# Two graph layers with attention and experts on one core: the bf16 copy of the adjacency made by casting transfers, attention products in quarters of the array, and an order of work read from a list

## The chip, the cores and the metric

The kernel runs on one core of a Trainium2 chip (trn2) as one program. The metric is the device time of that core in microseconds. The kernel before took 1467.53 us, the median of 3 runs (1466.63 to 1470.84).

The engines are named as in the profile: PE is TensorE (matmuls), PEld its weight loads, DVE is VectorE, ACT is ScalarE, POOL is GpSimd, SP is SyncE, which here issues DMAs only.

## The reference

There are N = 2708 nodes with 256 features and a matrix `adj` of 2708 x 2708 in float32, about 1.2% of it not zero, with values up to 1e9. Two layers follow one another; each is a graph part and an expert part.

```python
# layer 0
x = x + gnn0(layernorm(x), adj)          # softmax(leaky_relu(f1 + f2.T) + adj) @ h + bias
x = x + ffn0(layernorm(x))               # causal attention (4 heads, 2 key heads, 64 wide) over
                                         # 2708 tokens, then 8 experts, the best 2 for each token
# layer 1
x = x + gnn1(layernorm(x), adj)          # graph attention: mask = (adj != 0) | eye
x = x + ffn1(layernorm(x))               # 8 experts, the best 2 for each token
```

Since layer 0 adds `adj`, with its huge values, to the logits, the softmax of a row is one at the row's largest entry. The kernel finds that entry's index and gathers one row of `h`. (A general path for other data stands at the end of the program and is not taken.) Layer 1 needs only where `adj` isn't zero.

## The kernel before

The nodes lie in 22 tiles of 128 rows (the last has 20). There are four stages in order: `first` (layer 0's graph part, attention and routing), the experts of layer 0, `second` (layer 1's graph part and routing), the experts of layer 1.

**`first`**, for each pair of tiles in `project` and for each tile in `tile_in`:

1. `project`: statistics of x on DVE (`stats`), a power on POOL, transposes on PE (`turn`), `h` = x times the centred weights on PE (`times`, L949), scaled on ACT (`out_`) and stored to the DRAM tensor `hd`. The centred weights come from one PE product with `allones` (`centre`, L893 and L897).
2. `load` (SP, L990): one tile of 128 rows of `adj`, 10,832 bytes each, into one of three parts of `arena`.
3. `top` (DVE MAX8, L995) and `index` (DVE FIND_INDEX8, L999): the largest entry of each row and its place.
4. `narrow` (ACT, L1009) copies the tile to bf16 in two halves, with memsets of the padding on POOL (L1006, L1008), and `save` (SP, L1012) stores each half to the DRAM tensor `mb`. `narrow` needs the last store of `hd` to be issued. A part of `arena` is free for the next load when both `index` and `narrow` are done (the buffer names `adj0..2` and `low0..2`).
5. `fetch` (POOL, L1017): an indirect gather from `hd` that adds to x. It needs all of `hd`.
6. Statistics, norm, transposes, and the product with the query, key and value weights (PE, L1047); the rotation on POOL (L804 to L806, L1064); transposes into `qT` and `kT` (PE, L1070).

**Attention**, `pair(t0)`, for two tiles of queries t0, t0+1 against the tiles of keys up to t0+1, taken two at a time. For each tile of keys, `scores` multiplies 64 rows of `kT` and `qT` for each of the 2 key heads (PE, L1121: 64 rows, 128 columns, 512 wide, into the bank pair `st`), `exps` is on ACT (L1127), `mask` on POOL for the last two. `values` multiplies 128 rows of `V` and `e` into the bank `o` (PE, L1147: 128 rows, 64 columns for each key head). For the first three pairs (`PE_SUMS`) the softmax's sums are made by PE too (L1154, into bank `zs`); for the others DVE adds the tiles `e` up (`sums`, L1161 and L1166) and one PE product spreads the sums (L1199). Then `leave` copies `o` on ACT (L1188), DVE takes the reciprocal (L1204), POOL multiplies (`weigh`, L1208), PE projects (L1222), DVE and POOL add to x, and SP stores it. A product in float32 appears as two matmul instructions.

`route` runs after pairs 4, 10, 16, 18 and 20 (t0): logits (L424), the choice of two experts on DVE, and `send`, two indirect scatters for each tile on POOL (L1830) into the experts' lists `xs`. A few blocks of expert work (`early_blocks`) start within the stage. `nobody` (L1288) are PE fillers without use, put into gaps that the plan foresees; they multiply `allones` by `before`, a triangular matrix that DVE finishes (L232).

**The order of the work** around the change is set by `Plan`. Each step is added with an engine, an assumed length, what it needs, the buffers that it takes and gives, and a rank; `issue` then walks a model clock, and of the steps that can start soonest issues the one with the smallest rank. The instructions stand in the program in that order, each engine works its own in order, and semaphores keep the dependences:

```python
            soon = min(at for at, _ in can)
            first = min((s for at, s in can if at <= soon), key=lambda s: s["rank"])
```

**`second`** reads `mb` with transposing DMAs into bf16 masks, and aggregates over 22 tiles for groups of six (PE, L1603). It is ordered by a `Plan` of its own.

Of the kernel before, what the change touches and what calls it, by code (L numbers as in the profile page):

```python
# [20 lines left out]
P = 128  # L21
N = 2708
# [51 lines left out]

class Plan:
# [8 lines left out]
    UNIT = 0.24  # L84
    FILL = 0.75
    GAP_MIN = 1.0
# [38 lines left out]
    def issue(self, behind=0.0):  # L125
# [25 lines left out]
def adj_ffn_kernel(ctx, tc, x, adj, vecs, bias_rows, tab, w_gnn0, w_gnn1, wqkv, wo,  # L151
# [41 lines left out]

    ident = const.tile([P, P], F32, name="ident")
# [33 lines left out]
    allones = const.tile([P, P], F32, name="allones")  # L228
    nc.gpsimd.memset(allones, 1.0)

# [138 lines left out]

    def route(add, tiles, ready, copied, cleared, layer, XB, xs, pool, turn_tile, turn_bank, gate_tile, gate_bank, rank):  # L370
# [127 lines left out]
        if layer == 0:  # L498
            a = [add("ACT", 0.6, lambda t=t: squares(t), [ready[t - t0]], rank=rank) for t in tiles]
            a = add("DVE", 0.3, mean, a, rank=rank)  # L500
            scaled = add("POOL", 0.9, power, [a], rank=rank)
        last = None
        for pair in pairs:
# [10 lines left out]
            if gate_tile is None:  # L514
                a = add("ACT", 0.25, lambda pair=pair: keep(pair), [a], give=[turn_bank], rank=rank)
            last = a
        a = add("DVE", 3.2, choose, [last], rank=rank)
        b = add("ACT", 0.5, exps, [a], rank=rank)
# [3 lines left out]
        return [add("POOL", 2.7, lambda t=t: send(t), [b, c] + cleared, rank=rank + 6, lands=2.0) for t in tiles]  # L522


    def some_blocks(add, layer, blocks, fetched, needs, weights, xs, acc, new, named, rank):

        joins = []
        for k, (e, j, before) in enumerate(blocks):
# [68 lines left out]
            a = add("ACT", 0.7, back, [a], take=[names["xT"]], give=[names["mm"]], rank=r)  # L597
# [3 lines left out]
            a = add("ACT", 1.4, gate, [a], take=[names["sl"], names["hT"]], rank=r)  # L601
            a = add("DVE", 1.4, times, [a], give=names["up"] + [names["sl"]], rank=r)
# [4 lines left out]
            joins.append(add("POOL", 1.6, join, [a], give=[names["ys"]], rank=r))  # L607
        return joins

    def early_blocks(add, layer, needs, sent, *rest):  # L610
        blocks = [(e, j, (needs if layer == 0 else []) + sum([sent[t] for t in sent if t < before_t], []))
                  for e, j, before_t in EARLY[layer]]
# [196 lines left out]
    def first(X, XB, norms, tops, hd, mb, xs, acc, arena, load_weights):  # L809
# [11 lines left out]
        with ExitStack() as s:  # L821
# [24 lines left out]
            def tr_tile():  # L846
                return mm_tile().rearrange("p (k c) -> p k c", c=P)

            plan = Plan(mm=2, mv=4, ix=4, tb=6, st=2, o=1, zs=1, e=4, xg=3, hT=3,
                        z=2, qk=2, es=1, ob=2, yT=2, mb=2, rT=1, adj0=1, adj1=1, adj2=1, low0=1, low1=1, low2=1)  # L850
# [396 lines left out]
            for t in range(NT):  # L1247
                tile_in(t)
# [1194 lines left out]
```

## Time and profile before

| | us |
|---|---|
| Median of 3 runs | 1467.53 |
| The profiled execution, its own time | 1465.13 |
| Its span (first to last instruction) | 1463.3 |
| PE busy | 1385.9 (95%) |
| DVE busy | 775.9 (53%) |
| ACT busy | 555.3 (38%) |
| POOL busy | 525.3 (36%) |
| Granted TensorE clock, mean | 0.984 |

The busy shares are means over four stages with different limits; a stage is to be read from its own window. A busy PE is not PE at its peak: matmuls are pipelined, and a change of their shape costs time that the busy share doesn't show. The stages end at about 509.5, 804, 1148 and 1463.3 us.

### The profile page before, as it was taken

Reading aid. Unit: us, or ns where it says so; the run is one execution under the profiler, and the core shown is the slowest. Engines: PE = TensorE matmul, PEld = TensorE weight load, DVE = VectorE, ACT = ScalarE, POOL = GpSimd, SP = SyncE. Lnnn points to the kernel's source line nnn. Section 1 sums busy time; section 2 is a strip of 40 time slices with the busy share of each in tenths; the row PEclk is TensorE's granted clock in tenths of the full one; section 3 lists DMA queues with packets and bytes.
Section 4 is the critical chain, followed back from the end, with each engine's and each line's share of the span. In section 5 each row is a group of like instructions: output and inputs, shape, how many; then the busy total and the mean of one; then the engine's idle time right before and its main releaser. Section 6 shows DMA issues by size and latency. Waiting matters only on the chain.

```text
span 1463.3 us, 20902 instructions
## 1 busy us (share of the span) xinstructions
PE 1385.9 (95%) x7218; PEld 1006.3 (69%) x7218; DVE 775.9 (53%) x1680; ACT 555.3 (38%) x1104; POOL 525.3 (36%) x677
## 2 busy tenths in 40 slices
PE   6988989989999999999999899999999999999996
PEld 5643433433343888888788878888768888878885
DVE  5688999985676432222222474768565322322221
ACT  2576867655545322222221444434432211111110
POOL 5576668874224312222222210022334222222222
PEclk9899999999999999999999999999999999999998
DMA  7588756540001277777512770616321687666211
GB/s 268 192 290 287 252 197 226 158 155 31 8 16 64 46 205 185 168 175 197 105 18 26 159 166 1 133 39 151 108 73 58 148 214 187 194 185 129 24 19 21
DMA packets 260056, 193.05 MB, mean 132 GB/s; under 512 B 168008, under 2 KB 232104, under 8 KB 257232
## 3 DMA queue, kind: packets, MB, share of 16 engines
q1 hardware_dynamic: 235638, 162.32, 38.0%
q0 software_dynamic: 20032, 25.71, 9.7%
q10 hardware_dynamic: 4270, 3.58, 0.8%
q8 instruction: 59, 0.97, 0.3%
q14 instruction: 57, 0.47, 0.1%
HBM read 119.81 MB, written 56.11 MB: 120 GB/s over the span
## 4 chain that ended last, share of the span: by engine, by line
PE 77%; DVE 8%; POOL 6%; DMA 5%; issue 2%; ACT 1%; SPq 0%; POOLq 0%; DVEq 0%; ACTq 0%
PE pup L2115 23%; PE po L1603 15%; PE y L2130 13%; PE o L1147 4%; PE stt L1121 4%; PE up L562 3%; DMA X<-hd,ix 3%; PE pup L2146 3%; PE y L2180 1%; DVE yT L1204 1%; DVE es L1166 1%; PE po L949 1%; DVE ix L999 1%; POOL ra L804 1%; DVE tops L995 1%
## 5 line engine op out<-in xcount | busy, mean ns | idle before, releaser
L2115 PE MATMUL pup<-xTs,arena 128*128 128x256 f32 (+2 forms) x1320 | 249.7, 348 | 0.6 <-ACT xTs L2098 0.6
L2115 PEld LDWEIGHTS pup<-xTs,arena 128*128 128x128 f32 (+1 forms) x1320 | 218.5, 189 | 27.2 <-PE y L2180 1.5
L1603 PE MATMUL po<-hb,PT 128*128 128x257 f32 (+2 forms) x968 | 227.6, 389 | 2.9 <-DVE PT L1596 2.9
L2119 ACT ACTIVATE sl<-pup 128x256 f32<-128x256 f32 (+1 forms) x210 | 73.5, 350 | 368.9 <-PE pup L2115 325.4
L1603 PEld LDWEIGHTS po<-hb,PT 128*128 128x128 f32 (+2 forms) x968 | 176.7, 189 | 42.8 <-issue 13.3
L2120 DVE TENSOR_TENSOR hT<-sl,pup 128x256 f32<-128x256 f32 (+1 forms) x210 | 79.6, 380 | 225.8 <-ACT sl L2119 220.5
L1127 ACT ACTIVATE e<-stt 128x1024 f32<-128x1024 f32 (+1 forms) x132 | 125.5, 986 | 93.5 <-PE stt L1121 63.8
L1166 DVE TENSOR_TENSOR es<-es,e 128x1024 f32<-128x1024 f32 x104 | 137.8, 1325 | 29.8 <-ACT e L1127 22.0
L622 POOL DMA_INDIRECT out<-ys,XR x44 | 68.0, 1545 | 234.2 <-DVE ys L2133 149.5
L622 POOL DMA_INDIRECT acc<-ys,XR x44 | 68.3, 1553 | 215.4 <-DVE ys L2133 120.8
L1121 PE MATMUL stt<-qT,kT 64*128 64x512 f32 (+1 forms) x528 | 133.4, 616 | 4.3 <-ACT e L1127 3.9
L2130 PE MATMUL y<-arena,hT 128*128 128x256 f32 x612 | 137.3, 380 | 0.0
L2130 PEld LDWEIGHTS y<-arena,hT 128*128 128x128 f32 x612 | 114.6, 190 | 19.7 <-DVE hid L2154 4.9
L1830 POOL DMA_INDIRECT xs<-XR,place x88 | 93.2, 1059 | 91.8 <-DVE mk L1590 40.2
L1147 PE MATMUL o<-e,V 128*64 128x512 f32 (+1 forms) x528 | 122.4, 586 | 0.0
L1581 ACT ACTIVATE E<-sb,dcol 128x768 f32<-128x768 f32 (+1 forms) x88 | 75.3, 859 | 108.4 <-DVE PT L1596 106.5
L2133 DVE TENSOR_SCALAR ys<-y,XR 128x256 f32<-128x256 f32 x71 | 34.4, 484 | 133.7 <-PE y L2130 133.7
L2115 PE MATMUL pup<-xTs,room 128*128 128x256 f32 (+3 forms) x528 | 99.9, 346 | 0.0
L1121 PEld LDWEIGHTS stt<-qT,kT 64*128 64x128 f32 x528 | 44.7, 188 | 76.5 <-issue 63.0
L2115 PEld LDWEIGHTS pup<-xTs,room 128*128 128x128 f32 (+1 forms) x528 | 85.4, 189 | 9.8 <-PE y L2180 0.8
L1147 PEld LDWEIGHTS o<-e,V 128*64 128x64 f32 x528 | 32.9, 136 | 68.5 <-issue 53.2
L995 DVE MAX8 tops<-arena 128x8 f32<-128x2708 f32 (+1 forms) x22 | 65.3, 2970 | 1.5 <-DMA arena<-in_adj 1.5
(319 smaller groups left out, 1972.1 us busy)
## 6 DMA issues: line engine op xcount, KB each, us to landing
more<-in_w SPq DMA_DIRECT2D x48, 640.0 KB
arena<-in_adj SPq DMA_DIRECT2D x21, 1354.0 KB
arena<-in_w SPq DMA_DIRECT2D x36, 640.0 KB
mb<-mb SPq DMA_DIRECT2D x44, 352.0 KB
xs<-none SPq DMA_DIRECT2D x16, 536.0 KB
room<-in_w SPq DMA_DIRECT2D x12, 640.0 KB
pieces<-xs SPq DMA_DIRECT2D x200, 32.0 KB
acc<-X SPq DMA_DIRECT2D x21, 128.0 KB
```

Source lines behind the costliest of these rows:

```text
L622: i = nc.gpsimd.indirect_dma_start(out=acc[:, :], out_offset=bass.IndirectOffsetOnAxis(ap=tokens.bitcast(I32), axis=0), in_=ys, in_offset= ...
L995: nc.vector.max(out=tops[:r, t, :], in_=v["a"][:r])
L1121: nc.tensor.matmul(st[:r, g, c0(sb):], kT[a:b, sb * P:sb * P + r], qT[a:b, t0 + (sb == t0 + 1):t0 + 2, :, :], start=True, stop=True)
L1127: nc.scalar.activation(e[:r, :, c0(sb):], v[sb, "st"][:r, :, c0(sb):], AF.Exp, scale=1.0 / HD ** 0.5)
L1147: nc.tensor.matmul(v["o"][g * HD:(g + 1) * HD, c:], V[:r, sb, g * HD:(g + 1) * HD], v[sb][:r, g, c:], start=(n + i == 0), stop=(n + i == t ...
L1166: nc.vector.tensor_tensor(es, es, v[sb][:r, :, c:], ALU.add)
L1581: nc.scalar.activation(e[:q, :n], sb[:q, i0:i1], AF.Exp, bias=dcol[:q, j:j + 1], scale=SLOPE - 1.0)
L1603: nc.tensor.matmul(v["po", i][:r, :F], v["PT", j][:q, a:a + r], hb[:q, j, :], start=(j == 0), stop=(j == NT - 1))
L1830: i = nc.gpsimd.indirect_dma_start(out=xs[:, :], out_offset=bass.IndirectOffsetOnAxis(ap=at, axis=0), in_=src, in_offset=None)
L2115: nc.tensor.matmul(pp[:to, i, :B, :], wn[:, c, :], xT[:, c, :B, :], start=(c == 0), stop=(c == KC - 1))
L2120: nc.vector.tensor_tensor(hT[:, n, :B, :], sl[:, :B, :], pp[:, 1, :B, :], ALU.mult)
L2130: nc.tensor.matmul(y, hT[:, n, b, :], w[3][:, n, :], start=(n == 0), stop=(n == NHC - 1))
```

## The change

**Casting transfers, late.** `narrow` and `save` are gone. `cast` issues on POOL one DMA for each tile from `adj` in DRAM to `mb` in DRAM, float32 to bf16. All 22 need the last `load` in the plan, and each the one before it. `blank` stores the padding of `mb` once, on SP. The index goes into one tile `ixs` for all 22. An `arena` part is free after `index`.

**Quarters.** For all but the first three pairs, `scores` splits the keys of a tile in two halves of 64 columns, and `values` its rows in two halves of 64, so that both have the shape 64 rows by 64 columns. The second halves of `values` go to a second bank, `zs`, so that a pair takes `o` and `zs`. `leave` for these pairs is two DVE instructions, a copy of one bank and an addition of the other. `route` no longer uses `zs` for its logits but the turning bank and a copy (`keep`).

**Order.** Both plans take ranks from a list, `ORDERS[0]` for `first` and `ORDERS[1]` for `second`. Many assumed lengths differ, and some steps have added needs (the earlier choice of experts; the stores of x for the early blocks). Two steps without an instruction stand at each plan's end.

**Start.** x is loaded in five pieces, statistics and powers of `project` go by pairs of tiles, `tab` has a load of its own, and fillers multiply `allones` by itself; `allones` is set near the start of POOL's work. Fillers are counted with 0.22 for 0.24, 0.85 for 0.75 and gaps from 0.7 for 1.0.

```diff
+ORDERS = [[int(n) for n in text.split()] for text in (
...
-    UNIT = 0.24
-    FILL = 0.75
-    GAP_MIN = 1.0
+    UNIT = 0.22
+    FILL = 0.85
+    GAP_MIN = 0.7
...
+    def issue(self, order, behind=0.0):
+        for step, n in zip(self.steps, order):
+            step["rank"] = n
...
+            loads, ends = [], (2, 6, 14, NT - 1)
+            for a, b in zip((0,) + ends, ends):
...
-                def narrow(h):
-                    v["m", h] = m = adjp.tile([P, HALF], BF16, tag="mb", name="mb", bufs=2)
...
-                    nc.scalar.copy(m[:r, :b - a], v["a"][:r, a:b])
-                def save(h):
-                    nc.sync.dma_start(out=mb[t * P:(t + 1) * P, h * HALF:(h + 1) * HALF], in_=v["m", h])
+                def cast():
+                    nc.gpsimd.dma_start(out=mb[t * P:t * P + r, :N], in_=adj[t * P:t * P + r, :])
...
-                a = loaded[t] = add("SP", 5.8, load, take=[f"adj{t % 3}", f"low{t % 3}", "tb"], rank=rank,
-                                    lands=1.5)
+                a = loaded[t] = add("SP", 3.6, load, take=[f"adj{t % 3}"], rank=rank - 2.0, lands=2.0)
+                tb = add("SP", 0.4, load_tb, take=["tb"], rank=rank, lands=2.2)
...
+                def keys(sb):
+                    r = rows(sb)
+                    return [(0, r)] if on_pe else [(p, min(p + HD, r)) for p in range(0, r, HD)]
...
-                            nc.tensor.matmul(st[:r, g, c0(sb):], kT[a:b, sb * P:sb * P + r],
-                                             qT[a:b, t0 + (sb == t0 + 1):t0 + 2, :, :], start=True, stop=True)
+                            for p, q in keys(sb):
+                                nc.tensor.matmul(st[p:q, g, c0(sb):], kT[a:b, sb * P + p:sb * P + q],
+                                                 qT[a:b, t0 + (sb == t0 + 1):t0 + 2, :, :], start=True, stop=True)
...
-                                nc.tensor.matmul(v["o"][g * HD:(g + 1) * HD, c:], V[:r, sb, g * HD:(g + 1) * HD],
-                                                 v[sb][:r, g, c:], start=(n + i == 0), stop=(n + i == t0 + 1))
+                                for p, q in keys(sb):
+                                    to = v["o2" if p else "o"]
+                                    nc.tensor.matmul(to[g * HD:(g + 1) * HD, c:], V[p:q, sb, g * HD:(g + 1) * HD],
+                                                     v[sb][p:q, g, c:], start=(n + i == 0), stop=(n + i == t0 + 1))
...
-                    nc.scalar.copy(v["ob"], v["o"])
-                    if on_pe:
+                    if not on_pe:
+                        nc.vector.tensor_copy(v["ob"], v["o"])
+                        nc.vector.tensor_tensor(v["ob"], v["ob"], v["o2"], ALU.add)
+                    else:
+                        nc.scalar.copy(v["ob"], v["o"])
...
+            for t, cast in enumerate(casts):
+                last = add("POOL", 1.2, cast, [loaded[NT - 1], last], rank=NT + 0.5 * t, lands=6.0)
...
-                        nc.tensor.matmul(nobody[:, :P], allones, before, start=True, stop=True)
+                        nc.tensor.matmul(nobody[:, :P], allones, allones, start=True, stop=True)
...
-                plan.issue()
+                plan.issue(ORDERS[0])
```

## The prediction

> **What bounds the kernel now.** I read the page's busy shares first, then the windows by stage, the groups of the first stage, the waits of VectorE, and single matmuls. Four stages follow one another: the first (layer 0 up to its experts, 0 to 509.5 us), the experts of layer 0 (to 804), the second (layer 1 up to its experts, to 1148) and the experts of layer 1. The experts are untouched by the diff and TensorE is busy throughout them.
>
> The windows below cut the first stage at the ends of the 1st, 7th and 11th attention reciprocal (L1204, one for each pair of query tiles), and add the second stage. Columns: window, its length, then busy us (instructions) of PE, PEld, DVE, ACT and POOL, granted clock, DMA share, GB/s.
> ```profile
> 0.00:97.65 97.65, 74.96 (x374) 55.61 (x374) 65.82 (x132) 49.35 (x97) 61.30 (x115) 0.91 0.72 242
> 97.65:297.50 199.85, 179.74 (x798) 74.81 (x798) 189.86 (x185) 145.03 (x252) 150.57 (x192) 0.97 0.70 229
> 297.50:480.00 182.50, 174.29 (x796) 68.12 (x795) 124.38 (x170) 92.62 (x145) 77.18 (x105) 1.00 0.15 50
> 480.00:509.50 29.50, 27.05 (x192) 24.26 (x191) 10.79 (x45) 9.71 (x23) 12.79 (x17) 1.00 0.24 50
> 804.00:1148.00 344.00, 334.16 (x1773) 280.15 (x1774) 209.42 (x645) 136.93 (x251) 88.56 (x150) 0.99 0.41 99
> ```
> From 97.65 to 297.5 us VectorE is busy 95% of the time: it sets the pace there, TensorE is close behind. From 297.5 to 480 TensorE is (8.2 us idle; VectorE is busy 68%). In that second part the DMA engines lie nearly idle (share 0.15), in the first they carry 0.70.
>
> The groups show what fills the two engines:
> ```profile
> L1121 PE MATMUL stt<-qT,kT 64*128 64x512 f32 (+1 forms) x528 | 133.4, 616 | 4.3 <-ACT e L1127 3.9 <-issue 0.3
> L1147 PE MATMUL o<-e,V 128*64 128x512 f32 (+1 forms) x528 | 122.4, 586 | 0.0
> ```
> ```profile
> L1166 DVE TENSOR_TENSOR es<-es,e 128x1024 f32<-128x1024 f32 x104 | 137.8, 1325 | 29.8 <-ACT e L1127 22.0 <-issue 1.0 <-DVE es L1166 0.5
> L999 DVE FIND_INDEX8 ix<-tops,arena 128x8 uint32<-128x2708 f32 (+1 forms) x22 | 65.4, 2972 | 0.0
> L995 DVE MAX8 tops<-arena 128x8 f32<-128x2708 f32 (+1 forms) x22 | 65.3, 2970 | 1.5 <-DMA arena<-in_adj 1.5
> ```
> ```profile
> L1009 ACT CAST mb<-arena 128x1408 bf16<-128x1408 f32 (+3 forms) x44 | 57.2, 1323 | 5.6 <-DMA mb<-mb 4.6 <-POOL mb L1006 0.9
> ```
> VectorE's load is the row search (22 tiles, 5.94 us each) and the softmax sums. VectorE's waits before 300 us show where it is late:
> ```profile
> DVE st L268 <- DMA X<-hd,ix: 16.4, 8, 4.1
> DVE wgc L897 <- PE pm L893: 6.4, 1, 6.4
> DVE wq_sb L897 <- PE pm L893: 4.5, 1, 4.5
> ```
> The SP queue shows a further stall. Three adjacency tiles are loaded, and then none for 38 us, because a buffer is free only after its bf16 copy, and the copies wait for the last store of `hd`:
> ```profile
> 17.92 0.35 SPq L990 DMA_DIRECT2D arena<-in_adj  x1
> 21.72 0.33 SPq L992 DMA_DIRECT2D tb<-in_tab  x1
> 54.86 1.55 SPq L1012 DMA_DIRECT2D mb<-mb  x2
> 56.51 0.94 SPq L990 DMA_DIRECT2D arena<-in_adj  x1
> ```
> And TensorE's own timeline within the attention (start, length, line, form, count):
> ```profile
> 404.00 1.94 PE L1147 MATMUL o<-e,V 128*64 128x512 f32 x8
> 405.86 1.99 PE L1121 MATMUL stt<-qT,kT 64*128 64x512 f32 x8
> 407.78 0.39 PE L424 MATMUL pg<-rwn,rT 128*128 128x8 f32 x2
> ```
> Eight matmuls run as four waves of two: in the trace the two of a wave start 7 ns apart, and waves start 423 to 429 ns apart. Where the shape changes (128*64 to 64*128, or to 128*128) the next start is 519 to 523 ns away, 94 ns late, and the first wave in the new shape is longer: by 104 ns for 64*128, whose weights are no longer loaded under a running matmul, by about 47 ns for 128*64.
>
> **What the skill says.** "TensorEngine Tiling (Array Packing)", Key Properties: a change of tiling mode drains TensorE. The trace agrees, with the 94 ns. "TensorE: Matmul & The Clock Gate", Part 3: row and column tiling compose, and tiles at different places run concurrently. Here the trace shows rows alone (64*128), columns alone (128*64), and four column tiles (128*32, L1154: four starts 7 ns apart), never quarters. "DMA: Bandwidth & Descriptors", SWDGE vs HWDGE vs iDMA: a DMA that casts can be issued by GpSimd only, and only one software queue is allocated. The trace has no such cast. Its section Anatomy of one DMA prices a software DMA at 2.0 us plus bytes/436e3.
>
> **The change part by part.** I use durations of these rows and the instruction order that the two built programs show.
>
> *Casts off ACT and out of the loads' way.* Removed: 44 ACT casts (57.2 us), 23 POOL memsets (7.6 + 3.1 us), 44 stores of 352 KB on the SP queue. An adjacency buffer is now free after L999 alone. Gained is not ACT's time (it has slack) but the 38 us gap and the exps that stood behind a cast.
>
> Added: 22 casting DMAs from HBM to HBM, in the POOL order after the weigh of the 6th pair (about 245 us) and up to that of the 11th (453), when the DMA engines are idle. Their duration is unknown. Lower bound: a packet of one 10,832-byte row takes 480 ns in the adjacency loads; 8 rows on each of 16 engines make 3.84 us. Upper: at the rate of the accumulating gather (1,024 bytes in 110 ns), 9.3 us. The skill's price gives an estimate of 2.0 + 1387/436 = 5.2 us, which I take. 21.2 full tiles take 81 to 197 us of the 208 at hand, so the idle DMA time covers them. Their issue on POOL, at 1.7 us (the indirect gather, L1017), is 37 us where POOL is busy 77.2 of 182.5: hidden. Queued behind a cast on POOL are masks, weighs and the scatters of routed rows (L1830), behind it on the software queue scatters and the last gathers: up to one cast (5 us) later each. The last cast stands well ahead of the last scatters. If the cover is gone, see the fourth rival.
>
> *Start.* TensorE's fillers waited for `before` (9.29 us) and then held the transposes until 13.2, though x had landed at 5.6. They now multiply by an early memset, x comes in smaller pieces, and statistics go by pairs: I take 5 us off the start.
>
> *First stretch, to the 1st reciprocal.* In the new order VectorE has 73.3 us of work ahead of it (65.8 before: two more tiles are searched). Its idle time was 31.8 us; the waits of 6.4 and 4.5 go, and the buffer stall no longer starves it: I take 20. It ends at 93 (97.65).
>
> *Second stretch.* 176.7 us of VectorE work by the new order. I leave its 95%: 186 us, so the 7th reciprocal ends at 279 (297.5). TensorE has about 220 us of useful work by then: it fits.
>
> *Third stretch.* Of 182.5 us TensorE fills 3.3 with fillers and idles 8.2: 171 useful. Quarters: the order has 165 changes of shape before the experts where it had 219, 54 fewer at 94 ns (5.1 us); entries were 77 at 104 ns and 65 at 47, and become 9 at 104 and 77 at 47, quarters being priced as 64 columns (6.5 us): 11.6 in all. Pairs 8 to 11 hold 38 of the 60 steps in quarters: 7 us here; the order moves 2 us elsewhere: 162. The drain of `o` moves from an ACT copy (585 ns) to two VectorE instructions, 1.2 us by that same price, on both banks; behind it on VectorE are the sums, and the next pair's first values wait for both banks. TensorE has scores to run meanwhile: I take 0.9 us for each of 4 pairs, 3.5, between 0 and 10. Idle and fillers: 9 of 11.5 stay. Together 174.5: the 11th reciprocal ends at 453.5 (480).
>
> *Tail.* Reciprocal, weigh, projection, route, scatter, fetch: the same chain, 29.5 us. More fillers there (39 against 14) lie in waits. Stage end 483: 26.5 us earlier.
>
> *Second stage.* Same arithmetic, new order. TensorE is idle or filling for 9.8 + 9.3 = 19.1 us of 344. I take a quarter, 5, between -3 and 12.
>
> Sum: -31.5 us. Against the profiled execution (span 1463.3, time 1465.1) 1433.6; the median of the runs lies 2.4 above it: **1436**.
>
> **The rivals.** (1) The pace isn't there: VectorE keeps its idle time, the 10 us of drain work land on it, pair ends stall for the two banks. What stays is the start (5) and the fewer changes (11.6) less 4: 1455. For it: VectorE at 95%. Against: its waits above are ones that the change touches. 20%.
>
> (2) The search packs both stages well. In the first, TensorE is idle or filling for 86 us (509.5 less 423 useful): half of that, the changes of shape, and 8 in the second stage less some of the pair ends make about -55: 1413. Against: 35 of the 86 lie before the first scores, behind loads and `hd`. 17%.
>
> (3) Quarters don't run four at a time but two. Then 60 steps of 8 waves double: 60 x 8 x 0.43 = +206 us, about 1640. Against: four column tiles do run together. 2%.
>
> (4) Slower: the casts clog the software queue. The rows of layer 0's last tokens are scattered behind them, and POOL itself halts, since each software DMA of the built program waits for the eighth before it, with masks and weighs behind it. From 245 us on, 21.2 casts at 15 us last until 563, the experts start 10 us later: +63, 1530. It decides from 11.5 us a cast, (499 - 245)/21.2. Against: above the upper bound of 9.3. 7%.
>
> **How the numbers follow.** Forecast 50%, (1) 20%, (2) 17%, (3) 2%, (4) 7%, and 4% that gains and pair ends cancel. 0.3% is 4.4 us, about what a measurement of this kernel can tell. Faster 0.87, same 0.04, slower 0.09. The range reaches over (1) and most of (2), for the unknown pair ends and second stage: 1410 to 1464.
>
> **What would show it.** Right: quarters in waves of four 423 to 429 ns apart with no 94 ns between scores and values; adjacency loads without the gap at 22 to 56 us; the 7th reciprocal near 279, the 11th near 453, experts near 483. Wrong: casts that land over 11 us after issue, POOL waiting for DMA; waves 850 ns apart; TensorE waiting for VectorE's drain at each pair's first values.

## The result, and the profile after

The changed kernel takes **1461.49 us** (median of 12 runs, 1455.93 to 1465.33), the kernel before 1466.88 us beside it (12 runs, 1464.14 to 1470.84). The ratio is 0.9969 with a 95% interval of 0.9956 to 0.9981: about 5 us are gained where 31 were forecast. The profiled execution has a span of 1459.3 us and a time of 1461.3 us.

I cut it at the same events as before: the ends of the 1st, 7th and 11th attention reciprocal, here called R1, R7 and R11, and the first product of layer 0's experts. These are the windows of the changed kernel by stage; columns as before (window, length, busy us and instructions of PE, PEld, DVE, ACT and POOL, granted clock, DMA share, GB/s).

```profile
0.00:102.60 102.60, 82.68 (x445) 61.98 (x445) 75.56 (x127) 36.80 (x88) 58.29 (x101) 0.90 0.66 224
102.60:295.90 193.30, 174.01 (x1148) 69.09 (x1152) 181.20 (x198) 103.86 (x217) 142.42 (x172) 0.97 0.62 174
295.90:472.00 176.10, 166.21 (x1319) 63.76 (x1312) 134.62 (x168) 90.81 (x146) 95.48 (x126) 0.97 0.56 124
472.00:506.70 34.70, 33.82 (x257) 31.15 (x255) 12.03 (x46) 10.77 (x24) 14.15 (x24) 1.00 0.20 43
```
The second stage, from the end of layer 0's last expert product to layer 1's first, in the changed kernel and, in the second line, in the kernel before:
```profile
801.57:1142.08 340.51, 331.06 (x1786) 279.02 (x1787) 210.67 (x645) 136.44 (x251) 87.71 (x149) 0.99 0.42 100
803.29:1147.82 344.53, 334.02 (x1773) 280.04 (x1773) 209.91 (x646) 136.93 (x251) 88.56 (x150) 0.99 0.41 99
```

The two middle stretches are shorter (199.85 to 193.3 and 182.5 to 176.1 us). The first is longer by 5.0 us, and the last by 6.4 (28.3 to 34.7, from R11 to the experts' first product). The second stage is 4.0 us shorter, but in it 3.4 us ran at half the granted clock and before 10.2; what is left of the gain is worked out at the end. VectorE is still busy 94% between R1 and R7 (181.2 of 193.3).

The groups of the changed kernel: TensorE's quarters, VectorE's new drain, the short operation of the statistics that has grown, and POOL's casts.

```profile
L1225 PE MATMUL stt<-qT,kT 64*64 64x512 f32 (+4 forms) x1004 | 131.3, 604 | 5.7 <-ACT e L1231 5.6
L1255 PE MATMUL o<-e,V 64*64 64x512 f32 (+2 forms) x1004 | 121.9, 585 | 2.7 <-ACT e L1231 2.3 <-POOL e L1240 0.4
```
```profile
L1128 DVE SCALAR_TENSOR_TENSOR pv<-two_eps,mv 128x2 f32<-128x2 f32 x21 | 10.0, 475 | 0.8
L1298 DVE TENSOR_TENSOR osb<-osb,o 128x512 f32<-128x512 f32 x8 | 5.5, 688 | 0.8
L1297 DVE COPY osb<-o 128x512 f32<-128x512 f32 x8 | 5.5, 688 | 13.6 <-PE o L1255 13.6
```
```profile
L1115 POOL DMA_DIRECT2D mb<-in_adj x22 | 13.2, 626 | 0.0
```
Busy time by group says little of the quarters: 253.2 us against 255.8 before, since overlapping matmuls count once. TensorE's timeline says more:

```profile
331.68 1.95 PE L1255 MATMUL o<-e,V 64*64 64x512 f32 x16 [0.23 <-ACT e L1231]
333.45 1.04 PE L1225 MATMUL stt<-qT,kT 64*64 64x512 f32 x8
334.42 1.08 PE L1310 MATMUL pm<-es,allones 128*64 128x512 f32 x4
```
Sixteen matmuls in 1.95 us are four waves of four. In the trace the four of a wave start 5 to 8 ns apart, waves 428 to 430 ns apart at the median, and from values to scores the next wave also starts 429 ns on: the late 94 ns are gone. Only at the last line, where the shape does change, is the step from wave to wave 539 ns.

Two stretches lose, the start and the tail. First the start: the waits of the changed kernel ahead of R1 (engine, line, releaser: us in total, times, longest), of ACT, TensorE and VectorE in turn:

```profile
ACT hs L1065 <- DMA hd<-hs: 14.5, 2, 11.0
```
```profile
PE pm L1038 <- ACT wT L422: 9.1, 1, 9.1
```
```profile
DVE shift L459 <- PE pm L456: 8.2, 1, 8.2
DVE st L364 <- DMA X<-hd,ixs: 7.7, 1, 7.7
```
They are one chain. ACT writes two tiles of `hd` rows at a time into one of two buffers. It may not write the third pair before the first store has landed, 11 us. Behind it in ACT's order stands `wT`, a copy of transposed weights out of a bank of TensorE, which the new order has moved up; TensorE waits for that copy's bank, and VectorE for TensorE. The first accumulating gather, which needs every store, is issued at 56.5 us (53.0 before), and the first scores start at 84.2 (76.3). The kernel before had a wait of this kind too, a shorter one, and its `wT` came only at 51.1 us (28.8 in the changed kernel):

```profile
ACT hs L956 <- DMA hd<-hs: 6.0, 1, 6.0
```
SP's queue shows what the stores had to land behind:

```profile
9.74 0.33 SPq L1101 DMA_DIRECT2D arena<-in_adj  x1
...
14.56 4.04 SPq L1101 DMA_DIRECT2D arena<-in_adj  x2
...
34.73 0.34 SPq L1101 DMA_DIRECT2D arena<-in_adj  x1
```
The gap between adjacency loads is 16 us where it was 38.

### The profile page after: what moved, and what is told of

Its sections match the earlier page's. It is cut to its first block, busy times and chain, and to the rows that moved or that the text cites. A ratio compares the mean times of both kernels' runs of the same rounds, so it can differ in the third digit from the quotient of the medians.

```text
span 1459.3 us, 22759 instructions
## 1 busy us (share of the span) xinstructions
PE 1384.7 (95%) x8248; PEld 1010.1 (69%) x8248; DVE 790.5 (54%) x1686; ACT 500.4 (34%) x1063; POOL 531.6 (36%) x666
## 4 chain that ended last, share of the span: by engine, by line
PE 74%; DVE 10%; DMA 6%; POOL 5%; issue 2%; ACT 1%; SPq 0%; ACTq 0%; POOLq 0%; DVEq 0%
PE pup L2253 23%; PE po L1731 14%; PE y L2268 13%; PE stt L1225 4%; PE o L1255 3%; PE up L662 3%; PE pup L2284 3%; DMA arena<-in_adj 2%; POOL xs L1968 2%; DVE ixs L1111 2%; DVE yT L1315 2%; PE y L2318 2%; DVE tops L1108 1%; DMA hd<-hs 1%; DVE es L1274 1%
## 5 line engine op out<-in xcount | busy, mean ns | idle before, releaser
L1731 PE MATMUL po<-hb,PT 128*128 128x257 f32 (+2 forms) x968 | 222.8, 384 | 2.5 <-DVE PT L1724 2.5
L1225 PE MATMUL stt<-qT,kT 64*64 64x512 f32 (+4 forms) x1004 | 131.3, 604 | 5.7 <-ACT e L1231 5.6
L1968 POOL DMA_INDIRECT xs<-XR,place x88 | 97.4, 1107 | 105.8 <-DVE mk L1718 45.1
L1255 PE MATMUL o<-e,V 64*64 64x512 f32 (+2 forms) x1004 | 121.9, 585 | 2.7 <-ACT e L1231 2.3
L1255 PEld LDWEIGHTS o<-e,V 64*64 64x64 f32 (+1 forms) x1004 | 38.2, 136 | 71.4 <-issue 56.4
L1225 PEld LDWEIGHTS stt<-qT,kT 64*64 64x64 f32 (+2 forms) x1004 | 36.7, 138 | 65.8 <-issue 43.3
```

The lines of the kernel that those rows point to most:

```text
L1225: nc.tensor.matmul(st[p:q, g, c0(sb):], kT[a:b, sb * P + p:sb * P + q], qT[a:b, t0 + (sb == t0 + 1):t0 + 2, :, :], start=True, stop=True)
L1255: nc.tensor.matmul(to[g * HD:(g + 1) * HD, c:], V[p:q, sb, g * HD:(g + 1) * HD], v[sb][p:q, g, c:], start=(n + i == 0), stop=(n + i == t0 ...
L1731: nc.tensor.matmul(v["po", i][:r, :F], v["PT", j][:q, a:a + r], hb[:q, j, :], start=(j == 0), stop=(j == NT - 1))
L1968: i = nc.gpsimd.indirect_dma_start(out=xs[:, :], out_offset=bass.IndirectOffsetOnAxis(ap=at, axis=0), in_=src, in_offset=None)
```

## The experiments

All are edits of the changed kernel. Ratios are to the kernel before, measured beside each. The stages are from each run's trace, which is one execution: R1, the two stretches, and the tail from R11 to the experts' first product (in the kernel before that is 28.3 us; its window of 29.5 reached a microsecond further). "Half" is the time before the experts in which the granted clock was half.

| kernel | us | ratio (95%) | R1 | R1 to R7 | R7 to R11 | tail | half |
|---|---|---|---|---|---|---|---|
| before | | 1 | 97.7 | 199.8 | 182.6 | 28.3 | 27.3 |
| changed | 1461.5 | 0.9969 (0.9956 to 0.9981) | 102.6 | 193.3 | 176.1 | 34.7 | 44.4 |
| e1_whole | 1456.0 | 0.9923 (0.9901 to 0.9945) | 102.0 | 185.4 | 179.9 | 35.2 | 30.7 |
| e1_greedy0 | 1468.2 | 1.0008 (0.9993 to 1.0022) | 92.8 | 195.6 | 183.8 | 35.1 | 44.4 |
| e1_stores4 | 1449.6 | 0.9893 (0.9872 to 0.9914) | 93.2 | 189.3 | 176.1 | 34.6 | 30.7 |
| e1_adjlate | 1464.3 | 0.9978 (0.9965 to 0.9991) | 102.9 | 191.7 | 176.9 | 33.6 | 37.5 |
| e2_late_quarters | 1456.4 | 0.9930 (0.9914 to 0.9945) | 100.2 | 183.8 | 176.1 | 33.7 | 23.9 |
| e2_both | 1445.2 | 0.9857 (0.9839 to 0.9875) | 90.6 | 189.0 | 175.2 | 34.1 | 30.7 |
| e2_gate | 1462.0 | 0.9963 (0.9949 to 0.9976) | 99.0 | 194.6 | 176.3 | 34.2 | 44.4 |
| e2_casts_after | 1519.1 | 1.0365 (1.0342 to 1.0388) | 99.2 | 189.2 | 170.6 | 33.3 | 23.9 |
| e3_stores4_whole | 1455.6 | 0.9894 (0.9865 to 0.9923) | 90.4 | 185.6 | 180.4 | 35.1 | 30.7 |
| e3_drain | 1468.3 | 0.9986 (0.9968 to 1.0003) | 103.3 | 189.0 | 177.5 | 33.4 | 34.1 |
| e3_casts_early | 1473.6 | 1.0022 (1.0006 to 1.0038) | 101.6 | 192.0 | 179.8 | 33.6 | 44.4 |
| e3_best | 1456.1 | 0.9897 (0.9867 to 0.9927) | 93.0 | 188.0 | 182.5 | 33.2 | 44.4 |
| e4_nofill | 1443.5 | 0.9835 (0.9806 to 0.9864) | 89.6 | 187.3 | 176.0 | 32.8 | 25.2 |
| e4_tail | 1445.6 | 0.9846 (0.9817 to 0.9874) | 94.4 | 186.6 | 177.8 | 31.8 | 34.1 |
| e4_nofillers | 1447.5 | 0.9856 (0.9824 to 0.9888) | 89.6 | 186.9 | 177.6 | 33.5 | 47.5 |

The four runs whose names begin with e3 are a group apart: layer 1's attention products took 263 to 265 us in them, whatever the kernel (254 to 258 in the others, but for 258.5 in e2_casts_after), and the kernel before took 1471.1 us beside them. Why is not known; they bear the same chip number as the e2 runs. Their times are compared with each other, and their stages with the other runs.

How far single traces differ shows in kernels that share the program of a stretch:

- R1, with the written order: 99.0 to 103.3 us in the eight kernels with two buffers for the stores to `hd` (the first experiment explains them), 89.6 to 94.4 in the seven with four.
- R7 to R11, with the written order and the casts where they were: 175.2 to 177.8 us in the ten kernels with quarters there, 179.9 and 180.4 in the two without.
- The tail: 33.4 to 35.2 us in the nine kernels that left it alone.
- Half clock: layer 1's attention products took 254.4 us where none of it fell on them, 256.0 to 256.1 with one piece of 3.4 us and 257.4 to 257.7 with two (changed kernels outside e3). A piece costs about 1.6 us there.

Two profiled executions lie off their medians: that of e2_late_quarters is the fastest of its six (1451.5 us, median 1456.4), that of e3_best the slowest of its six (1462.8, median 1456.1).

**The stores' buffers (e1_stores4).**
```diff
-v["hs"] = ab.tile([P, 2 * W2], F32, tag="osb", name="hs")
+v["hs"] = ab.tile([P, 2 * W2], F32, tag="osb", name="hs", bufs=4)
```
(the other tile of that tag alike)

> The changed kernel with four buffers instead of two for the rows that ACT stores to hd; every engine's order unchanged. Theory A (the start is lost because ACT waits 11.0 and 3.5 us for a store to land before it may write the third and a later pair, with the turned weights and TensorE's transposes behind it): ACT's waits fall below 5 us in all, TensorE's 9.1 us wait for wT goes, the first gather starts at 48 to 52 us instead of 56.5, R1 near 95 instead of 102.6, and 4 to 7 us of it reach the end: 1455 to 1458. Rival B (the stores land late whatever the buffers, because the adjacency loads are in the DMA queues before them, and the next wait ends at the same time): first gather within 2 us of 56.5, time within 2 us of 1461.5.

Theory A, and more of it than expected. The first gather starts at 44.4 us instead of 56.5, R1 comes at 93.2, and 12 us reach the end. This is its window to R1, and the one to R7:

```profile
0.00:93.20 93.20, 80.70 (x445) 60.60 (x445) 76.33 (x127) 36.89 (x88) 58.41 (x101) 0.93 0.73 246
93.20:282.50 189.30, 172.94 (x1166) 68.62 (x1164) 179.82 (x198) 104.65 (x217) 140.06 (x172) 0.98 0.64 178
```
VectorE does the same 76 us of work in 93 us instead of 103. The same tag holds the attention's drained products, but not before the first pair's end, where R1 lies; so what the start lost was lost in the wait for a buffer. The two traces also differ by 6.8 us of half clock ahead of R1, which can make 3.4 of the 9.4 us at most, and the two ranges of R1 given above lie apart. Of the 12 us some lie between R1 and R7 (193.3 to 189.3), where half clock fell by 6.3 us; that part was not separated.

**The loads in front of the stores (e1_adjlate).**
```diff
-nc.sync.dma_start(out=v["a"][:r], in_=adj[...])      # tiles 1 and 2
+nc.scalar.dma_start(out=arena[...], in_=adj[...])    # behind the 5th and 7th hd store
```


> The changed kernel with the loads of the 2nd and 3rd adjacency tile moved from SP (14.6 and 18.3 us) to ACT's queue behind the 5th and the 7th hd store; every engine's order otherwise unchanged. Theory A (the two loads, which VectorE needs only from 49 us on, stand in the DMA engines before the hd stores): the stores of the first pairs land in under 6 us instead of 12, TensorE's 9.1 us wait falls below 4, first gather at 48 to 53 us, R1 near 96, time 1454 to 1458. Rival B (the search now waits for its tiles instead): VectorE waits over 4 us for the adjacency before 70 us, R7 within 2 us of 295.9, time within 2 us of 1461.5 or above.

Rival B. The early stores land sooner, but ACT still waits 9.0 us for them (in three waits), and the moved loads now meet the last stores: the first gather goes from 56.5 to 61.3 us, and VectorE gets a wait for the adjacency. These are ACT's and VectorE's waits ahead of R1 in this kernel:

```profile
ACT hs L1065 <- DMA hd<-hs: 9.0, 3, 6.5
```
```profile
DVE tops L1113 <- DMA arena<-in_adj: 4.6, 1, 4.6
```
Moving the loads only moved the wait; with four buffers ACT waits 1.2 us for landings in all, and that paid.

**The quarters (e1_whole, e2_late_quarters, e2_both, e3_stores4_whole, e3_drain).**
```diff
-return [(0, r)] if on_pe else [(p, min(p + HD, r)) for p in range(0, r, HD)]
+return [(0, r)]                         # e1_whole, e3_stores4_whole
+return [(0, r)] if t0 < 14 else [...]   # e2_late_quarters, e2_both
```
and where products are whole, `nc.scalar.copy(v["ob"], v["o"])` instead of the drain on VectorE.

> The changed kernel, but every product of the attention whole again (64*128 scores, 128*64 values, one bank for o, which ACT copies out); order, fillers and casts as in the changed kernel, instruction for instruction. Theory A (the quarters bring what was forecast, and the gain was lost elsewhere: at the start, the tail and in the second stage): 54 more changes of shape at 94 ns and dearer first waves, less the drain of two banks on VectorE, make it 6 to 10 us slower than the changed kernel: about 1469 us, the third stretch (7th to 11th reciprocal) 182 to 184 us instead of 176.1. Rival B (what the quarters save comes back at the pair ends or as stretches of half clock, of which the changed kernel's trace shows more): within 2 us of 1461.5, the third stretch within 2 us of 176, and the granted clock back at 0.984 from 0.979.

Neither theory. Without quarters the kernel is faster, by 0.46% of the kernel before. The windows of e1_whole between R1, R7 and R11 say where:

```profile
102.00:287.40 185.40, 173.95 (x755) 69.89 (x755) 171.93 (x190) 106.39 (x221) 139.01 (x170) 0.97 0.65 180
287.40:467.30 179.90, 173.02 (x753) 64.57 (x753) 131.18 (x159) 92.39 (x150) 94.02 (x129) 0.98 0.56 122
```
Behind R7, where TensorE sets the pace, quarters save 3.8 us (179.9 to 176.1); the forecast had 7 less 3.5 for the pair ends. Ahead of it, where VectorE sets it, they cost 7.9 by these two traces (185.4 to 193.3): VectorE's busy time to R7 is 256.8 us with them and 249.2 without, of which the drain of four pairs, 688 + 688 ns each, makes 5.5. The saved changes of shape do not make up for that. Over all kernels with the written order and two buffers the sign stands, not the size: 189.2 to 194.6 us in five with early quarters and this drain, 185.4 and 183.8 in the two without.

> The changed kernel with quarters only from the 8th pair on; the 4th to 7th pair multiply whole arrays, and ACT copies their one bank out, at the places of the old drain. Theory A (the stretch from the 1st to the 7th reciprocal is set by VectorE, so there the drain of two banks costs and the saved changes of shape pay nothing; behind the 7th TensorE sets the pace and they pay): the second stretch as with no quarters, 185 to 187 us instead of 193.3, the third as with quarters, 175 to 177.5 instead of 179.9; together 1451 to 1455 us. Rival B (the second stretch's 8 us with quarters came from something that all variants share by chance, such as stretches of half clock): second stretch 190 us or more, time within 2 us of 1456 to 1461. Rival C (what is saved early is lost at the switch, since the 8th pair starts from two banks that the 7th did not use): third stretch 179 us or more, time near 1456.

> Quarters from the 8th pair on, and four buffers for the rows stored to hd. Theory A (the two losses are separate: one lies before the 1st reciprocal, the other between the 1st and the 7th): gains add, R1 near 93, R7 near 278, R11 near 454.5, time 1440 to 1444 us. Rival B (an earlier start only moves VectorE's waits into the second stretch): less than 4 us below the 1449.6 us of the four buffers alone.

By the stages of e2_late_quarters, theory A: 183.8 and 176.1 us, the better half of both kernels. Its windows:

```profile
100.20:284.00 183.80, 171.17 (x778) 68.45 (x779) 171.88 (x189) 106.27 (x221) 139.06 (x170) 0.99 0.66 182
284.00:460.10 176.10, 165.84 (x1339) 63.30 (x1339) 135.37 (x168) 91.06 (x146) 96.96 (x129) 0.98 0.59 126
```
But these are of its fastest execution. Its time, 1456.4 us, is that of e1_whole and above the 1451 to 1455 expected, so the 3.8 us do not show in the time.

Together with four buffers (e2_both) it is 1445.2 us, 4.4 below the four buffers alone and 1 above the expected range. Where these 4.4 us lie is not shown. The stretch to R7 is 189.0 us, as good as with early quarters and four buffers (189.3 in e1_stores4), and VectorE waits 5.7 us for TensorE's sums in it, 1.5 in e2_late_quarters; 2.6 us lie ahead of R1, where the two kernels are the same. With four buffers the early quarters thus cost less, if anything: 189.3 us with them, 185.6 to 189.0 in six kernels without.

> Four buffers for the rows stored to hd, and no quarters at all. Theory A (quarters are worth 3 to 4 us from the 8th pair on, where TensorE sets the pace): 3 to 4 us above the 1445.2 us of quarters from the 8th pair on with the four buffers, third stretch 179 to 180 us against 175.2. Rival B (in the time they are worth nothing anywhere): within 2 us of 1445.

The third stretch is as expected (180.4 against 175.2), and the ratio, 0.9894 against 0.9857, points to theory A; but the intervals overlap, and e3 is a group apart. Nor is it different from e1_stores4, which has four buffers and quarters from the 4th pair on (0.9893): there the quarters, early and late together, are worth nothing in the time. Whether late quarters are worth 4 us in the time stays open. That early ones cost is shown with two buffers (0.9930 in e2_late_quarters against 0.9969, and the intervals do not meet), not with four.

> The changed kernel with quarters in all pairs from the 4th; the first bank of o is copied out by ACT, and VectorE only adds the second: 0.73 us of its work for each pair instead of 1.42. Theory A (the quarters' loss between the 1st and the 7th reciprocal is VectorE's own work, as it sets the pace there): VectorE's busy time there 178 to 179 us instead of 181.2, the stretch 190 to 191 us instead of 193.3, the third stretch unchanged. Rival B (it is the wait for both banks, and VectorE's work only fills it): stretch within 1 us of 193.3, or longer, as a second engine's step comes between.

Between R1 and R7 VectorE is busy 175.9 us, and the stretch is 189.0 us: on theory A's side, by more than expected and by more than the copies that went, 4 times 688 ns, can explain. It is one trace: e2_casts_after, with the whole drain, has 178.9 and 189.2 us there. The ratio to the kernel before, 0.9986, does not show the gain. Against rival B speaks that VectorE waits only 1.0 us for the banks in this stretch of the changed kernel, and 3.4 us for ACT's copy in e3_drain. So VectorE's own work is the likelier cause, but this experiment alone does not show it.

**The casts (e2_casts_after, e3_casts_early).**

> The changed kernel with all 22 casting transfers issued by POOL behind the last scatter of layer 0 instead of between 258 and 460 us. It tells what they cost where they were, in the first stage; what they cost among the experts is a separate question. Theory A (in the third stretch and the tail they are hidden): third stretch 175 to 177 us, tail 34 to 35 us. Rival B (they hold up POOL's queue or the software queue, and so the scatters): third stretch or tail shorter by 3 us or more. The experts of layer 0: 5 to 30 us longer if their scatters and accumulating transfers on POOL stand behind 22 casts of 7 us, else unchanged.

In the first stage rival B: with the casts gone from it the third stretch is 170.6 us, 5.5 shorter:

```profile
288.40:459.00 170.60, 164.30 (x1328) 62.48 (x1321) 134.42 (x168) 90.92 (x146) 85.23 (x108) 0.99 0.18 58
```
Part of it is a wait of TensorE that is gone in this kernel: for the expert rows fetched behind the scatters of token tiles 12 to 17, which share the software queue with the last casts (TensorE's waits of the changed kernel, R7 to R11):

```profile
PE pm L640 <- DMA XR<-xs: 3.5, 1, 3.5
```
The rest may be clock: 0.99 of it was granted there, 0.97 in the changed kernel (4.2 us at half clock against 10.7). In the changed kernel 6.8 us of half clock begin while TensorE is in that wait (columns as before; 0.91 us busy in the first line):

```profile
460.24:463.65 3.41, 0.91 (x12) 0.03 (x4) 3.27 (x4) 0.00 (x0) 0.00 (x0) 1.00 0.56 116
463.65:470.48 6.83, 5.58 (x19) 3.23 (x20) 2.12 (x2) 1.76 (x6) 4.06 (x7) 0.50 0.27 93
```
The experts pay for the move: those of layer 0 take 358.2 us instead of 294.9, 63 more where at most 30 were expected, and the kernel is 57 us slower. These are waits of POOL and of TensorE in e2_casts_after from 492 us on:

```profile
POOL mb L1115 <- DMA mb<-in_adj: 41.5, 14, 5.4
```
```profile
PE pup L2253 <- DVE hT L2258: 50.3, 2, 46.2
```
Twenty-two casts in a row halt POOL itself, 14 times, each until an earlier one has landed. Spread out as in the changed kernel, none of them waited (the 0.0 in its group).

> The changed kernel with the last four of the 22 casting transfers issued with the 9th, 13th, 17th and 18th of them, ahead of 440 us, so that none stands among the scatters of the tokens 12 to 17 (440 to 470 us). Theory A (the casts' cost in the first stage is that these scatters land late behind them, and TensorE waits 3.5 us for the expert rows fetched after them): that wait falls under 1 us, third stretch and tail together 206 to 208 us instead of 210.8, time 3 us below 1461.5. Rival B (what they cost is shared DMA time or half clock): together within 1.5 us of 210.8.

The wait of 3.5 us goes, as theory A says, but the stretch and the tail are 213.4 us, which neither theory had, and a longer wait has come, for ACT's exponentials (TensorE's waits from 293 us on):

```profile
PE stt L1225 <- ACT e L1231: 7.6, 3, 6.6
```
Theory A saw the first wait only. POOL then ran its scatters without a pause from 440 us on, and ACT, whose buffers are handed on through POOL's work, may have waited for those; that link was not tried. Where they are, the casts cost the first stage up to 5.5 us, and this place is no better.

**The order (e1_greedy0).** The list of the first stage left out: `plan.issue(None)`.

> The changed kernel without the written-out order of the first stage: the planner orders it by its ranks and lengths; casts, quarters, pieces of x stay. Theory A (the searched order is worth the part of the gain that came, and costs at the start, where it was searched on a model that has no late landing of the hd stores): the first gather within 3 us of 56, R7 later than 296 by 3 to 10 us, time 1464 to 1472. Rival B (the written order is itself what loses the start and the tail): experts start earlier than 506.7 by 4 us or more, time below 1457.

The time is theory A's, the places are not. By these traces the written order is worth 2.3 us between R1 and R7 and 7.7 us between R7 and R11, and it loses 9.8 us ahead of R1, where the planner's own order keeps the folds out of the way: ACT waits 12.8 us for stores there too, but the first copy `wT` comes at 46.9 us (51.1 in the kernel before, 28.8 in the changed one), and the first gather at 48.9. The two reach the experts within 0.6 us of each other. Of the 4.5 us between the two profiled executions 3.8 lie in the second stage, which is the same program with 10.2 us of half clock against 3.4; so the time does not tell what the order is worth. The second stage's list changes nothing: with it left out, the program gives every engine the same instructions in the same order.

**The tail (e2_gate, e4_nofill, e4_tail, e3_best, e4_nofillers).** This is the chain of waits of the changed kernel, ahead of its experts:

```profile
489.01 3.58 PE up L662 x32
...
492.62 0.61 ACT chunks L670
493.23 1.33 issue
494.55 0.95 POOL xs L1968
...
498.41 3.70 DMA xs<-XR,place
```
All 32 products of an expert block stand ahead of the ranks, from which the last rows' places come. In the kernel before it was 16 (L468 is the ranks' first product):

```profile
494.95 1.78 PE up L562 x16
496.73 0.13 PE pg L468 x2
```
And this is the end of the same chain in e2_both:

```profile
482.98 4.69 PE nobody L1418 x42
487.67 0.12 PE y L2367 x2
487.80 0.50 PE pt L2233 x4
```
The rows' load was issued at 483.9, and the transposes `pt` follow at once when 42 records of fillers (21 matmuls) end.

> The changed kernel, but the last route of layer 0 has its gate logits in the bank of their own that they had in the kernel before (the bank zs), without the ACT copy; the rest of the order unchanged. Theory A (the tail is 5 to 6 us longer because the gates stand in the two banks that the expert blocks' products also use): from the 11th reciprocal to the experts' first product 31 to 32 us instead of 34.7, time 1458 to 1459. Rival B (the tail is longer for another reason, the order of the expert blocks' products or the scatters' landing): 34 to 35 us, time within 2 us of 1461.5.

Rival B: the tail is 34.2 us. The shared bank is not the cause.

```diff
-add("PE", 0.5, lambda: None, [a], rank=999.0)
+add("SP", 0.0, lambda: None, [a], rank=999.0)    # no wait of TensorE to fill
```


> Quarters from the 8th pair on and four buffers, without the last group of fillers ahead of layer 0's experts (21 matmuls on allones, which run until just before the experts' first transposes); the order is otherwise unchanged. Theory A (the tail is longer because those fillers, planned for a wait of 4 us that is not there, hold TensorE while the experts' rows have already landed): the transposes start 2 to 2.5 us after the rows' load is issued, as in the kernel before (2.1 us), instead of 3.7; tail 32 to 33 us against 34.1. Rival B (the rows land no earlier than the fillers end): tail within 0.5 us of 34.1.

> The same, and the two matmuls of the last ranks ahead of the second half of one expert block's products. Theory A (both stand in one chain: the ranks 1.8 us late, then the fillers): tail 30 to 31 us against 34.1, nearly the 28.3 of the kernel before, time 3 to 4 us below the 1445.2 us of quarters from the 8th pair with four buffers. Rival B (the landing of the scatters sets the end): tail 32.5 us or more.

The transposes now start 2.1 to 2.2 us after the rows' load is issued, as in the kernel before, and in e4_tail's chain the load stands where the fillers did:

```profile
487.02 2.13 DMA XR<-xs
489.15 0.04 issue
489.19 0.86 PE pt L2238 x4
```
The tails are 32.8 and 31.8 us, below every tail that was left alone (33.4 to 35.2): both steps are in the chain, by 1.3 and 1 us in these single traces. That is not half of the loss, and 31.8 is above theory A's 30 to 31; where the other 3.5 us lie was not taken apart. In the time e4_tail is no better than e2_both (0.9846 against 0.9857). e4_nofill has the best median, 1443.5 us, and gives back some at once: 6.8 us of half clock start at 484.4, and from the experts' start to layer 1's first attention product it takes 343.2 us, e2_both 340.7.

> Quarters from the 8th pair on, four buffers for the stores to hd, the last four casts issued earlier, and in the tail the two matmuls of the ranks moved ahead of the second half of one expert block's products. Theory A (the tail is longer by 1.8 us because all 32 products stood ahead of the ranks, and the casts cost 3 us): third stretch and tail together 204 to 206 us against 209.3, time 1440 to 1442 us. Rival B (the tail's end is set by the landing of the scatters, not by when the ranks come): the tail within 0.7 us of 34.1, time 1442 to 1445.

The time is 1456.1 us, level with e3_stores4_whole beside it, and the third stretch and the tail are 215.7 us instead of 204 to 206. This is its slowest execution, with 17.1 us of half clock between R7 and R11 (6.8 in e2_both), and the new wait of e3_casts_early is in it. In the tail the last rows' load is issued 26.4 us after R11 (29.1 in e2_both), but fillers held the transposes for 5.6 us after that: most of the ranks' gain of 2.6 us was eaten by the next thing in the chain.

> Quarters from the 8th pair on and four buffers, with no fillers at all in the first stage. Theory A (all but the last group lie in waits and change nothing): only the tail is shorter, by 1 to 2 us, and R1, R7 and R11 stay within 2 us of 90.6, 279.6 and 454.8. Rival B (fillers keep the granted clock up): the stretches of half clock before 490 us grow from 30.7 us to over 45, and R1 is later by 3 us or more.

Mixed. The half clock grows to 47.5 us, as rival B says, but R1 is not later, as theory A says, and the ratio, 0.9856, is that of e2_both. The tail, 33.5 us, is not the 1 to 2 us shorter that theory A expected; 6.5 us of half clock lie in it.

## Why the prediction was wrong, by its own steps

It forecast 1433.6 us for the profiled execution, which took 1461.3. The forecast missed by 9.6 us at the start, 7.3 to R7, 1.6 to R11, 5.2 in the tail and 3.8 behind it.

- **Start: the sign was wrong.** VectorE's idle time before R1 was taken from 31.8 to 20 us because its two waits for centred weights would go. They went, but the idle time is 27.0 us, and the work 75.6 instead of 73.3. The failed step is "the buffer stall no longer starves it": the adjacency's buffers were meant, and the stores' buffers were overlooked. ACT already waited 6.0 us for them in the kernel before; I read VectorE's and TensorE's waits there, not ACT's. Four buffers give R1 at 93.2, against 93 forecast; that it meets so closely is luck, since 76.3 us of work and 16.9 of idle time stand there for 73.3 and 20.
- **R1 to R7.** I kept VectorE at 95% of 176.7 us of work. The share held (94%); the term that failed is the work, 181.2. The drain had been counted, at 1.2 us a pair; it takes 1.38. The statistics' `pv` takes 475 ns on average instead of 344. More important, I reckoned the quarters' gain over the stage and never asked what they cost alone where VectorE sets the pace: 7.9 us by the first two traces.
- **R7 to R11: right in sum, in part by luck.** 176.1 against 174.5. The quarters' 7 less 3.5 for pair ends is 3.8 as measured, but the stall at the pair ends is not in TensorE's waits, and 10.7 us of half clock in the changed kernel against 6.2 in e1_whole can hide 2.2 us of what the quarters save. The order, taken at 2 us, is worth 7.7 by e1_greedy0. Against it stand 3.5 us for rows behind a cast and that half clock, up to 5.4 us of time; the forecast had neither, and the kernel before had no half clock here. So too low a gain and left-out losses met. The 94 ns were a little low: 523 is counted from a wave's last start and 429 from its first; like for like the changes of shape from 404 to 411 us come 97 to 100 ns late.
- **Casts.** The estimate of 5.2 us from the Trainium skill ("DMA: Bandwidth & Descriptors", Anatomy of one DMA) was low: the median from issue to landing is 7.3 us for full tiles, from 5.8 to 12.7, and the measurement decides. Of the 16 whose landing is recorded four pass my upper bound of 9.3 us, and two, with another cast or the clearing stores of `mb` beside them, my point of 11.5 (by its own sum, 254/21.2, it is 12.0). Their issue takes 626 ns on POOL, not 1.7 us. "Queued behind a cast ... up to one cast (5 us) later each" is what the 3.5 us wait shows; I named it and gave it no price.
- **Tail.** "The same chain, 29.5 us" failed (34.7), and so did "More fillers there (39 against 14) lie in waits": the last group held TensorE, and one block's products went ahead of the ranks.
- **Second stage.** The forecast of 5 us rested on "new order", and the list changes nothing there. The trace shows 344.5 us before and 340.5 now, but with 10.2 and 3.4 us of half clock. Eight kernels with the same second stage and 10.2 us of it have 342.2 to 344.4, the other one with 3.4 (e1_whole) 339.2. So 1 us or so is the program's, the rest the clock's. Behind it layer 1's experts take 317.3 us instead of 315.5, with 2.0 us more of half clock.

The rival nearest to the result is the first, at 1455: VectorE does keep its pace and takes the drain. It still counted on the start's 5 us. The fourth names a real mechanism, POOL halting behind casts, which e2_casts_after set off. The quarters do run four at a time, so the third is out.

All seven kernels with four buffers beat both (0.9835 to 0.9897). The two lowest ratios are those of quarters from the 8th pair on without the last fillers (0.9835) and of that with the ranks moved as well (0.9846); their intervals overlap, with each other and with that of e2_both (0.9857).

## What to carry to other kernels

Before you price a change of an engine's work, ask in which stretch that engine sets the pace: here the same edit lost 7.9 us in one stretch and gained 3.8 in the next, because what it saved was TensorE's and what it spent was VectorE's. Compare such numbers over several traces: with four buffers the loss was hardly to be seen. Read the waits of the engines that seem to have slack, too: an in-order engine that waits for a store's buffer holds everything that a new order has put behind it. Fillers are planned for a wait; when the wait goes, they become the delay.

## What the runs showed of the hardware that I had not expected

- The granted clock falls to half in pieces of about 3.4 us. Before the experts these make 27.3 us in the kernel before, 44.4 in the changed one, and 24 to 48 over all kernels. The kernels with quarters from the 4th pair on have 24 to 44, those without 31. In the changed kernel the seven stretches of it before the experts begin at 23.3, 43.8, 64.3, 180.3, 293.0, 351.0 and 463.7 us, and in the 3.4 us ahead of these TensorE was busy 11, 43, 35, 55, 39, 5 and 27% of the time; in the kernel before, at 29.3, 53.2, 70.2, 128.3 and 223.8 us, it was 0, 64, 39, 49 and 39%. So there half clock mostly follows a stretch in which TensorE waits, and a wait costs more than its length. It is not the whole rule: in the kernel before, two pieces in layer 1 begin at 927.0 and 1053.3 us, behind 3.4 us in which TensorE was busy throughout. At half clock 17 us more are up to 8.5 us of TensorE's time, and in layer 1's products a piece did cost about 1.6 us. No run held it still, so it stands beside every difference of a few microseconds between two traces here.
- Quarters (64*64) of one wave start 5 to 8 ns apart, and scores follow values with no late start.
- A casting transfer of 677 KB costs POOL 626 ns on average when they are spread out, and 22 in a row halt it 14 times, up to 5.4 us each.
